# Pinning every engine's queue to the order in which a planner traces the kernel

## The chip, the cores and the metric

One core of a Trainium2 chip runs the whole program. Its engines are TensorE (PE, with its weight loads as PEld), VectorE (DVE), ScalarE (ACT), GpSimd (POOL) and SyncE (SP, which only issues DMAs here). Times are device microseconds (us) of one execution; lower is better.

## The reference

The input x has 32 rows (batch) of 128 tokens by 128 features, in float32. Two layers are added to it.

```python
x = x + L0_ffn(L0_cond(x, cond_512, ...), ...)
x = x + L1_ffn(L1_cond(x, ids, mask, cond_512, cond_64, fside, ...), ...)

# L0_cond: kx = modulated_linear(x); per token attention among 16 heads of 8
#          features, q = k = v = kx; then another modulated linear
# L0_ffn:  gates choose and weight experts out of 16 (at least the two best);
#          q, k, v = weighted sums over the chosen experts' projections;
#          attention over blocks of 256 tokens as reshaped; output projection
#          again by the same experts
# L1_cond: layer norms whose gain and shift are looked up by ids, three small
#          MLPs of the row's state, all joined in a last MLP and a layer norm
# L1_ffn:  top 2 of 8 experts, each silu(x W_gate) * (x W_up) through W_down
```

The kernel computes only the experts that are chosen. It counts whether more than two would be needed anywhere, and has a second version for that case, which does not run on these inputs.

## The kernel before, in words

The 32 rows are handled in 4 parts (p0 to p3) of 8 rows, and inside a part in groups of 4 rows (g0 to g7 over the whole batch). A part passes through these stages:

- *front0*, per group, on two lanes: the modulated linear and the per-token attention of layer 0's condition. Its large DVE operations are prod (scores) and prodv (weights times values), with a sum over prodv taken by PE transposes (pat).
- *gates0* and *route*: a chain of short DVE operations, with a matmul (prk) in it that ranks tokens. Its links after prk are blk, upto, first, row_at, pick, row_plf and at last place, the row of a sorted buffer to which every token goes. The same numbers, clamped, are back.
- *send*: 16 indirect DMAs from POOL that scatter the part's rows into rows_x in HBM, sorted by expert and padded to blocks of 128 rows, 28 blocks per part.
- *experts0*: SP loads the blocks (crx), PE transposes them (pcrx) and multiplies by the block's expert (qkv), ACT copies the result (yx), and SP writes it (outs_x).
- *attend0*, per row, on three lanes: POOL gathers both experts' results (gq), ACT and DVE weight and add them, PE does the attention (psc, ppT, pov), ACT copies (prT and others), and POOL scatters the result to rows_o.
- *output0*: blocks again, cro, yo, outs_o. Then *add_up*: POOL gathers (ygo), DVE adds to X.
- *front1*, per group, on two lanes, after all groups of front0: the condition of layer 1, from the transposes pyT to the logits pl.
- *gates1*, *route*, *send* to rows_c (crow is what is sent), *experts1* with loads crc, gate and up matmuls gu, their product hh, its transposes phT, the down matmuls yc and the writes outs_c, 22 blocks per part; and add_up again with ygc, after which SP writes the output.

Each stage is a Python generator. A planner, the class `Turns`, runs the one that by its own count can begin first, and the calls that the generator makes until its next `yield` are traced. Every call goes through a wrapper, which keeps that count (`account`, with a cost for each kind of instruction):

```python
def call(out, *args, **kw):
    turns.account(name, op, out, args, kw)
    return fn(out, *args, **kw)
```

All instructions are issued from the wrapper, so the profile gives nearly all of them the same line, L237; they are told apart by their tiles.

## Time and profile before

| | |
|---|---|
| median of 3 runs | 1030.94 us |
| lowest and highest | 1025.16 and 1032.98 us |
| the profiled execution: time | 1030.12 us |
| its span, from first to last instruction | 1028.2 us |
| granted TensorE clock, mean | 0.774 of full speed |
| PE, DVE, ACT, POOL busy | 618.9, 481.4, 392.0, 390.7 us |
| DMA | 118.24 MB, 115 GB/s over the span |

The busy time of an engine is the time in which at least one of its instructions ran. The slices in the page's second part each stand for a fortieth of the span, 25.7 us, and a digit gives the busy share in tenths. A wait line names the engine that waits and the tile that its next instruction writes, then what released it, the total, the number of times and the longest. A timeline line gives start and length in us, the engine, the operation, and in brackets the idle time ahead of it with its releaser. "Remote", and "another core or an unknown queue", mean that the profile shows no releaser.

### The profile page before, as it was taken

The numbers are of one execution on the slowest core, as the hardware profiler recorded it, in microseconds if no ns is written. First come the engines' busy times: TensorE is split into PE (matmuls) and PEld (weight loads), VectorE is DVE, ScalarE is ACT, GpSimd is POOL, SyncE is SP. The second block draws the span as 40 slices with busy tenths as digits, with TensorE's granted clock in tenths as the row PEclk, the third lists the DMA queues.
The fourth block names the chain that finished last, engine by engine and source line by source line (L and its number), as shares of the span: only waits on it lengthen the run. The fifth ranks groups of instructions, "written<-read, shape, count | busy, mean of one in ns | idle before, by whom it ended". The sixth has DMA issues, their size and how long they took to land.

```text
span 1028.2 us, 11024 instructions
## 1 busy us (share of the span) xinstructions
PE 618.9 (60%) x3050; PEld 435.7 (42%) x3050; DVE 481.4 (47%) x1625; ACT 392.0 (38%) x1016; POOL 390.7 (38%) x399
## 2 busy tenths in 40 slices
PE   5366536855962863555672583285959569469570
PEld 3245424543742642533451461173536346246340
DVE  6878772972893550022432454253646435032212
ACT  3232132714641452333662482162536225135240
POOL 0000061075027247365557457705321640741405
PEclk9976567965995886686886675678989789769885
DMA  8990014323324465554654342352121221232212
GB/s 231 322 266 1 0 31 143 134 81 108 133 103 128 123 202 170 145 172 138 208 174 133 105 139 62 117 158 73 65 74 49 60 78 54 79 102 59 66 51 61
DMA packets 144604, 118.24 MB, mean 115 GB/s; under 512 B 11416, under 2 KB 133720, under 8 KB 144536
## 3 DMA queue, kind: packets, MB, share of 16 engines
q1 hardware_dynamic: 130200, 83.88, 26.8%
q0 software_dynamic: 14336, 33.58, 11.2%
q8 instruction: 28, 0.46, 0.2%
q14 instruction: 40, 0.33, 0.1%
HBM read 57.38 MB, written 60.03 MB: 114 GB/s over the span
## 4 chain that ended last, share of the span: by engine, by line
PE 32%; issue 13%; DVE 13%; POOL 12%; another core or an unknown queue 10%; DMA 10%; ACT 5%; SPq 3%; POOLq 0%; ACTq 0%; DVEq 0%
POOL rows_x L237 6%; PE gu L237 5%; PE yc L237 4%; PE pat L237 3%; PE qkv L237 3%; DVE prodv L237 3%; SPq L237 3%; PE pre L237 2%; POOL gq L237 2%; PE phT L237 2%; DMA gq<-outs_x,back 2%; POOL rows_o L237 2%; PE yo L237 2%; POOL ygc L237 1%
## 5 line engine op out<-in xcount | busy, mean ns | idle before, releaser
L237 POOL DMA_INDIRECT rows_x<-h,place x64 | 70.1, 1095 | 202.9 <-DVE past L237 132.1
L237 POOL DMA_INDIRECT gq<-outs_x,back x64 | 68.6, 1072 | 146.5 <-PE pov L237 67.4
L237 POOL DMA_INDIRECT ygc<-outs_c,back x64 | 60.8, 949 | 127.9 <-DMA outs_c<-ycs 97.7
L237 PE MATMUL qkv<-w,crTx 128*128 x224 | 96.2, 545 | 14.6 <-issue 4.9
L237 PE MATMUL gu<-w1e,crTc 128*128 x176 | 100.0, 657 | 5.8 <-DVE hh L237 3.8
L237 POOL DMA_INDIRECT rows_c<-crow,place x64 | 62.1, 970 | 72.3 <-ACT hT L237 36.3
L237 PE MATMUL pat<-ident,prodv 128*128 128x128 f32 x512 | 70.5, 301 | 22.7 <-DVE prodv L237 17.6
L237 DVE TENSOR_TENSOR prodv<-S,kx 128x2048 f32<-128x2048 f32 x32 | 72.4, 2287 | 24.7 <-PE pat L237 24.6
L237 POOL DMA_INDIRECT ygo<-outs_o,back x64 | 61.2, 956 | 59.2 <-DVE hh L237 28.2
L237 PEld LDWEIGHTS pat<-ident,prodv 128*128 128x128 f32 x512 | 65.5, 157 | 29.6 <-issue 17.3
L237 DVE TENSOR_TENSOR hh<-hh,gu 128x256 f32<-128x256 f32 x88 | 36.6, 418 | 88.1 <-ACT hh L237 68.6
L237 POOL DMA_INDIRECT rows_o<-orow,place x64 | 65.5, 1024 | 19.5 <-issue 15.8
L237 PE MATMUL yc<-w1e,hT 128*128 x352 | 55.0, 299 | 24.1 <-ACT hT L237 19.9
L237 PEld LDWEIGHTS yc<-w1e,hT 128*128 128x128 f32 x352 | 49.9, 211 | 32.8 <-ACT hT L237 23.8
L237 ACT COPY yx<-qkv 128x384 f32<-128x384 f32 x112 | 50.4, 490 | 27.3 <-PE qkv L237 13.7
L237 PE MATMUL phT<-ident,hh 128*128 128x128 f32 x176 | 35.7, 292 | 38.3 <-DVE l1t L237 11.0
L237 DVE SCALAR_TENSOR_TENSOR gq<-gq,w 128x384 f32<-128x384 f32 x32 | 19.7, 616 | 81.7 <-DMA gq<-outs_x,back 36.2
L237 PEld LDWEIGHTS qkv<-w,crTx 128*128 128x128 f32 x224 | 41.9, 214 | 34.4 <-issue 13.4
L237 PEld LDWEIGHTS phT<-ident,hh 128*128 128x128 f32 x176 | 24.2, 151 | 69.8 <-issue 48.5
L237 ACT ACTIVATE hh<-gu 128x256 f32<-128x256 f32 x88 | 34.3, 390 | 47.0 <-PE phT L237 28.0
L237 PE MATMUL pcrx<-ident,crx 128*128 128x128 f32 x112 | 22.4, 329 | 46.2 <-DMA crx<-rows_x 44.9
L237 DVE TENSOR_REDUCE nm<-psc 128x1 f32<-128x128 f32 x32 | 9.2, 289 | 76.9 <-remote 24.1
(289 smaller groups left out, 1417.2 us busy)
## 6 DMA issues: line engine op xcount, KB each, us to landing
outs_x<-yx SPq DMA_DIRECT2D x56, 384.0 KB
crx<-rows_x SPq DMA_DIRECT2D x28, 256.0 KB
cro<-rows_o SPq DMA_DIRECT2D x28, 256.0 KB
outs_o<-yos SPq DMA_DIRECT2D x28, 256.0 KB
crc<-rows_c SPq DMA_DIRECT2D x20, 256.0 KB
outs_c<-ycs SPq DMA_DIRECT2D x20, 256.0 KB
rows_x<-zeros SPq DMA_DIRECT2D x6, 512.0 KB
rows_o<-zeros SPq DMA_DIRECT2D x6, 512.0 KB
```

What stands on the lines that cost most here:

```text
L237: return fn(out, *args, **kw)
```

## The change

At every call, before the new instruction is traced, a new method `pin` looks through what was traced since the last call. It gives each instruction on one of the five engines an edge to the instruction traced before it on the same engine. The edge is of order alone: no semaphore belongs to it. Within a group of scatters to the same buffer no edges are made; what follows the group has an edge to each of them. The wrapper calls `pin`, and `scatter` tells the planner its group. Nothing else changes: not the calls, their sizes, the buffers or the planner's costs.

```diff
+    ENGINES = {
+        getattr(mybir.EngineType, n) for n in ("PE", "Activation", "DVE", "Pool", "SP")
+    }
...
-    def __init__(self, nc):
+    def __init__(self, tc):
+        nc = self.nc = tc.nc
+        self.tc, self.seen, self.last, self.groups = tc, 0, {}, {}
...
                 def call(out, *args, **kw):
+                    turns.pin()
                     turns.account(name, op, out, args, kw)
                     return fn(out, *args, **kw)
...
+    def pin(self):
+        traced = self.nc.cur_bb.bb.instructions
+        for i in traced[self.seen:]:
+            if i.engine not in self.ENGINES:
+                continue
+            group = self.groups.get(i.name)
+            before, run, of = self.last.get(i.engine, ([], [], None))
+            if group is None or group != of:
+                before, run = run, []
+            for name in before:
+                self.tc.add_manual_dep(
+                    i, name,
+                    mybir.DependencyInfo(mybir.DependencyClass.NoSync, mybir.DependencyReason.DATA),
+                    reason="in the order of tracing",
+                )
+            self.last[i.engine] = before, run + [i.name], group
+        self.seen = len(traced)
...
-    tn = Turns(nc)
+    tn = Turns(tc)
...
         tc.add_to_no_dep_group(group, ins.ins)
+        tn.groups[ins.ins.name] = group
```

The instructions are the same 10690 before and after; they stand in another order on all five engines.

## The prediction

> **What bounds the kernel now.** I read the page's busy line first, then the waits, then the chain of work that ended last, then engine timelines where a wait was long.

> ```profile
> PE 618.9 (60%) x3050; PEld 435.7 (42%) x3050; DVE 481.4 (47%) x1625; ACT 392.0 (38%) x1016; POOL 390.7 (38%) x399
> DVE  6878772972893550022432454253646435032212
> ...
> PE 32%; issue 13%; DVE 13%; POOL 12%; another core or an unknown queue 10%; DMA 10%; ACT 5%; SPq 3%; POOLq 0%; ACTq 0%; DVEq 0%
> ```

> No engine is full: the busiest, PE, works 60% of the span. DVE's slices of 25.7 us say that for the first 12, to about 300 us, it is 7 to 9 tenths busy, and later 2 to 6. The chain passes through every engine. So the time is set by when one stage hands over to the next, which is what an order decides. The waits name the hand-overs (us in total, times, longest):

> ```profile
> POOL rows_x L237 <- DVE past L237: 132.1, 1, 132.1
> POOL ygc L237 <- DMA outs_c<-ycs: 97.7, 3, 37.5
> ...
> POOL gq L237 <- issue: 63.7, 49, 49.0
> ...
> PE pcrx L237 <- DMA crx<-rows_x: 44.9, 4, 21.2
> ```

> POOL can't scatter part 0's rows until DVE has routed them at 134 us, and the expert matmuls can't start until the rows have come back. The end of part 0's routing, in DVE's timeline (start, length):

> ```profile
> 123.97 0.17 DVE L237 CAST blk<-blk_i 128x16 f32<-128x16 int32 x1
> 124.45 2.29 DVE L237 TENSOR_TENSOR prodv<-S,kx 128x2048 f32<-128x2048 f32 x1 [0.31 <-PE pat L237]
> 126.66 0.18 DVE L237 TENSOR_TENSOR_SCAN upto<-blk 128x16 f32<-128x16 f32 x1
> 126.76 1.33 DVE L237 TENSOR_TENSOR prod<-kx 128x1152 f32<-128x1152 f32 x1
> 128.01 0.17 DVE L237 TENSOR_TENSOR first<-upto,blk 128x16 f32<-128x16 f32 x1
> ...
> 134.08 0.17 DVE L237 CAST place<-row_plf 128x16 uint32<-128x16 f32 x1
> ```

> Each short link of the route waits behind a 1.3 to 2.3 us operation of the next group's attention, which nobody needs yet: 10.1 us from blk to place. Part 3's route, with less beside it, takes 381.80 to 384.17, or 2.4 us, for the same links. The timelines of PE, DVE and ACT after 400 us show the other kind of loss:

> ```profile
> 416.70 0.79 PE L237 MATMUL pov<-gq,prT 128*128 128x128 f32 x2 [10.70 <-ACT prT L237]
> ...
> 417.18 0.62 DVE L237 SCALAR_TENSOR_TENSOR gq<-gq,w 128x384 f32<-128x384 f32 x1 [13.47 <-ACT prT L237]
> ...
> 415.88 0.62 ACT L237 ACTIVATE gq<-gq,w 128x384 f32<-128x384 f32 x1 [11.70 <-DMA gq<-outs_x,back]
> ```

> Here ACT's queue holds the scaling of a gather (gq) ahead of prT, a copy whose input was there at 404. The gather sits on POOL behind part 3's scatter. PE, DVE and ACT all stand for 10.7 to 13.5 us.

> [...] one copy with its input ready waited 11.7 us behind its predecessor. So an order fixed badly costs as much as one fixed well saves. [...] part 0's last scatter record starts at 157.35 and lasts 0.96, and the chain carries another 2.24 us of DMA up to 160.9. [...] rows_x scatters have a mean of 1095 ns, those of part 0 reaching 2.02 us beside DVE's attention, while ygc gathers have 949 ns.

> **The change part by part.** [...] The added edges are of order alone on one engine, so they put no new wait into the program; their cost is only what stands behind whom. I sum against the profiled execution, 1030.12 us (span 1028.2); the median of the three runs, 1030.94, is 0.8 above it and I ignore that.

> *Routing of the first layer.* I listed what stood ahead of each part's place on DVE and no longer does, with durations from the trace: 19.0 us for part 0 (four prodv of 2.3, prod and S of 1.3 each, a softmax of 3.0), 13.8 for part 1, 13.7 for part 2, 5.0 for part 3; nothing is newly ahead. Of part 0's 19.0 I count 17: about 2 us of DVE's idle time comes to light as the links hop to PE and back (the chain shows 0.99 us of "issue" at 114.3 for one such hop). Part 0's place falls from 134.1 to about 117. The work moved behind it fits beside the scatter and the load, 31 us (135.1 to 166.0) paced by POOL and the DMA queues. Expert matmuls start at about 149 instead of 166.

> *PE and SP there.* The next group's pk and pkx (138 to 143 before) now stand behind the first experts' transposes. They wait for rows that land at about 146, so they lose some 5 us, inside the 24 us that part 1 gains. SP now issues the second layer's weight loads (5.8 MB) and the zero fills of rows_c between the first loads of experts; at the 231 to 322 GB/s of the first slices 5.8 MB are 18 to 25 us of DMA, spread over a stretch at 69 GB/s. I take 3 us; the bounds are 0 and 20.

> *POOL, parts 0 to 2.* Before, part 1's scatters (221.6) stood behind six gathers that waited 49 us for outs_x. Now twelve of the sixteen stand ahead. With place at about 190, twelve at 1.27 us (0.96 and a gap of 0.30) end at 206, so gq of row 0 comes at 207: no gain against 208.6. The other four end at about 215 instead of 244.6. Part 2's sixteen still stand before gq of row 4, but come about 38 us earlier, so part 0's attention, which ended at 387, does too, and its output experts start near 360 instead of 398.6.

> *The second layer's start.* It gets back only part of this. The gathers for the residual (ygo of rows 1 to 3 of part 0, run at 449 to 462) now stand behind gathers of part 2, row 3's behind one run at 503.4 to 505.7. If those come 38 us early, ygo of row 3 ends near 470 and front1's first group starts some 14 us earlier than 486. With the later groups, for which POOL is less in the way, I carry 24 us into the second layer.

> *Second layer.* front1's eight groups run on two lanes from 486 to 867, a group taking 52 to 92 us from its first transpose to its logits, and the last route (872.1) follows them. On PE the instructions traced ahead of part 2's and part 3's place are 33.0 and 29.4 us (summed durations, which overlap) less than what had run by then. The page's busy time is about 0.6 of such sums, so 18 us less stands ahead of the last route: 18 us. The stall at 404 goes, since the prT concerned is traced ahead of that gather: 13 us, of which nothing is sure to remain if the gather itself is late next.

> *Tail.* What no longer stands ahead must run after: 18 us of PE work, in a tail where PE was busy 75.7 of 128 us after 900; I let 10 of it show. The last scatter on POOL (14 of part 3's 16) moves behind part 1's sixteen ygc gathers, from 875.6 to after about 920 less the shift. Its rows were needed at 941.7 when gu of part 3 began, and 14 times 1.27 plus 3 to land is 21: in balance with PE, which was at part 2 until 938. I take 0, bounds 0 and 20.

> Sum: -24 - 18 - 13 + 10 = -45; 1030 - 45 = 985 us.

> **The rivals.** *Slower: the front of the second layer dams up the experts on PE.* gu 15 of part 0 ran at 761.9, while the logits of front1's group 5 (pl), now traced ahead of it, ran at 792.8. PE will have to wait for them. Nothing is lost if that group comes 31 us earlier; if it gains only the first route's 17, all expert work behind is 14 us late, and the displaced PE work adds to the tail: 1030 + 14 + 4 = 1048 us; with no gain 1065. For it: 31 us of ready matmuls filled PE's gaps before. Against it: front1's own instructions lose the same work ahead of them.

> *Nothing measurable.* The gain goes into the waits at ygo and at ygc (97.7 us), which end with transfers: 1030. For it: gq of row 0 gains nothing by the sum above. Against it: every route is freed, not one.

> *More.* 10% of the chain has no visible releaser; from 556.15 DVE stands 15.26 us for the largest of these pieces, and the reduction that ends it, at 571.43, had its input at 567.1. If such stalls come from the mixture of POOL's bursts with waiting queues, and the order dissolves half of these 103 us as well, the time is 985 - 50 = 935 us. Nothing shown ties them to the order.

> That the edges do nothing is no case: the queues differ in hundreds of places.

> **How the numbers follow.** Forecast 985 with its own range 955 to 1015: 0.50. More gain: 0.12. Nothing: 0.11. Slower: 0.27. Within 1% is about what a measurement of this kernel can tell from no change, 1021 to 1041. The range 930 to 1055 takes in both rivals' centres and leaves out some 0.07 below and 0.11 above. Faster 0.62, same 0.11, slower 0.27.

> **What would show it.** Right: place of part 0 near 117 with its links 0.2 to 0.5 us apart; first qkv near 149; part 1's scatter ending near 215; no common gap of PE, DVE and ACT of over 10 us near part 3's scatter; the last route near 820. Wrong: front1's first group no earlier than 486, gu of part 0 waiting on pl for over 15 us, or PE idle before part 3's first gu for its rows.

## The result, and the profile after

The changed kernel takes 1020.12 us (median of 20 runs, 1014.31 to 1029.15) against 1029.38 us for the kernel before beside it (20 runs, 1022.02 to 1035.77). The ratio is 0.9915, with a 95% interval of 0.9889 to 0.994: a gain of 0.85%, real but a fifth of the 45 us that were forecast. The profiled execution has a span of 1012.8 us, 15.4 less than before.

The page of the kernel after, in the order in which before was read: busy time, DVE's slices, the shares of the chain that ended last.

```profile
PE 637.9 (63%) x3050; PEld 447.2 (44%) x3050; DVE 526.7 (52%) x1625; ACT 394.9 (39%) x1016; POOL 398.9 (39%) x399
DVE  6797986979976500121454463566666534221312
...
DVE 27%; PE 26%; another core or an unknown queue 15%; issue 13%; ACT 8%; SPq 4%; DMA 4%; POOL 3%; ACTq 0%; DVEq 0%; POOLq 0%
```

POOL and DMA, 12% and 10% of the chain before, are down to 3% and 4%. What has grown is time with no visible releaser: 153 us of the chain against 106 before. The 47 us more are as much as the forecast gain. In a second pair of traces of the two kernels (further down) it grows from 89 to 116 us: the direction is the same, the size is not. The waits that the lists put down to "remote" agree: they add up to 172.6 us before and 213.1 after, in the second pair to 155.1 and 193.6. Some lines of the list after (us in total, times, longest):

```profile
POOL rows_x L243 <- DVE past L243: 118.9, 1, 118.9
DVE hh L243 <- ACT hh L243: 91.1, 50, 13.9
POOL ygc L243 <- DMA outs_c<-ycs: 69.5, 3, 29.3
...
POOL rows_c L243 <- ACT ycs L243: 51.9, 1, 51.9
...
DVE l0st L243 <- remote: 33.0, 2, 23.7
```

The start-up wait is 13.2 us shorter, as forecast in kind. The largest "remote" wait stands where a DVE chain of front1 (l0st) begins.

In the first layer the order did what was expected of it. The end of part 0's route in DVE's timeline:

```profile
116.25 1.22 DVE L243 TENSOR_REDUCE hm<-S 128x64 f32<-128x1024 f32 x1
117.50 1.22 DVE L243 TENSOR_TENSOR S<-S,hm 128x1024 f32<-128x1024 f32 x1
118.64 0.17 DVE L243 TENSOR_SCALAR blk_i<-prk 128x16 int32<-128x16 f32 x1
...
119.05 0.17 DVE L243 CAST blk<-blk_i 128x16 f32<-128x16 int32 x1
119.26 0.19 DVE L243 TENSOR_TENSOR_SCAN upto<-blk 128x16 f32<-128x16 f32 x1
119.49 0.17 DVE L243 TENSOR_TENSOR first<-upto,blk 128x16 f32<-128x16 f32 x1
...
120.93 0.17 DVE L243 CAST place<-row_plf 128x16 uint32<-128x16 f32 x1
```

From blk to place it is now 1.9 us instead of 10.1, with the same links next to each other. Start times from the timelines of the two kernels, by stage:

| | before | after | difference |
|---|---|---|---|
| place of part 0 | 134.1 | 120.9 | -13.2 |
| place of part 1 | 214.0 | 195.5 | -18.5 |
| place of part 2 | 301.3 | 269.1 | -32.2 |
| place of part 3 | 384.2 | 343.8 | -40.4 |
| first cro of part 0 | 398.6 | 355.4 | -43.2 |
| pyT of the first front1 group | 486.4 | 490.4 | +4.0 |
| second layer's place, part 0 | 629.9 | 602.0 | -27.9 |
| part 2 | 811.9 | 763.1 | -48.8 |
| part 3 | 872.1 | 841.1 | -31.0 |
| last ygc gather | 1018.7 | 1005.2 | -13.5 |

The lead grows to 43 us, is lost before front1 starts, comes back, and falls to 13.5 us in the last two stretches. The largest wait without a releaser stands in the middle of part 3's output and front1. ACT's timeline there:

```profile
616.85 1.14 ACT L243 ACTIVATE act<-pre,b1T 128x128 f32<-128x128 f32 x4 [4.67 <-PE pre L243]
617.86 1.65 ACT L243 ACTIVATE xk<-X,l1nb,l1y 128x128 f32<-128x128 f32 x4
621.12 0.59 ACT L243 COPY q<-pyT 128x512 f32<-128x512 f32 x1 [1.62 <-remote]
630.98 0.59 ACT L243 COPY crTo<-pcro 128x512 f32<-128x512 f32 x1 [9.27 <-remote]
640.22 0.59 ACT L243 COPY q<-pxh 128x512 f32<-128x512 f32 x1 [8.66 <-remote]
```

and in DVE's at the same time:

```profile
640.16 0.30 DVE L243 BATCH_NORM_STATS2 l0st<-py 128x6 f32<-128x128 f32 x1 [23.67 <-remote]
```

PE's timeline has what they wait for:

```profile
617.53 0.66 PE L243 MATMUL pcro<-ident,cro 128*128 128x128 f32 x4 [0.29 <-DMA cro<-rows_o]
...
619.37 0.22 PE L243 MATMUL py<-b2row,ones_b 96*128 96x128 bf16 x1
```

PE's last matmul into py ends at 619.59. DVE, with nothing else to do since 616.49, starts to read py at 640.16: 20.6 us after its input was complete by the record. ACT reads pcro 12.8 us after its matmuls ended at 618.19, though it was free from 621.71. SyncE, whose next cro load waits until PE has read cro for that same pcro, goes on at 630.97 too. So it is the signal of PE that comes late, not one engine that sleeps.

The trace shows this directly, since it also keeps the time of each semaphore update: each wait of ACT and DVE above that is put down to "remote" ends 0.02 us after an update of PE's, so that update is the signal here. Taken in the order of PE's queue, the update for pcro, due at 618.19, is recorded at 630.96, and the one for py, due at 619.59, at 640.14. The next four, due between 622.88 and 634.54, follow within 0.27 us.

Some updates are missing from this trace: 613 of PE's 718 are on record, and all engines and DMAs together have 7594, where a trace of the same kernel without late signals (below) has 13634. The first of PE's to go missing, 3 of 18, are due between 100 and 150 us, and POOL's first sixteen indirect DMAs run there, from 122.0 to 148.0.

To count the late starts, I call a start late if the instruction begins over 1 us after both the end of the last instruction whose signal it waits for and the end of the instruction before it on its engine. The sums add up over engines and need not lie on the critical chain, and they depend on how the source of a signal is found: if it is taken to be the last PE instruction on the same tile, the 250.3 us of the changed kernel's first trace in the table below become 191.4 and its third trace stays at 0.

### The profile page after: what moved, and what is told of

Its sections match the earlier page's. It is cut to its first block, busy times and chain, and to the rows that moved or that the text cites. A ratio compares the mean times of both kernels' runs of the same rounds, so it can differ in the third digit from the quotient of the medians.

```text
span 1012.8 us, 11074 instructions
## 1 busy us (share of the span) xinstructions
PE 637.9 (63%) x3050; PEld 447.2 (44%) x3050; DVE 526.7 (52%) x1625; ACT 394.9 (39%) x1016; POOL 398.9 (39%) x399
## 4 chain that ended last, share of the span: by engine, by line
DVE 27%; PE 26%; another core or an unknown queue 15%; issue 13%; ACT 8%; SPq 4%; DMA 4%; POOL 3%; ACTq 0%; DVEq 0%; POOLq 0%
PE gu L243 5%; SPq L243 4%; PE pat L243 3%; PE qkv L243 3%; PE yc L243 3%; DVE S L243 3%; DVE prodv L243 2%; POOL rows_x L243 2%; DVE prod L243 2%; PE phT L243 1%; DVE X L243 1%; PE pre L243 1%; DVE l1t L243 1%; DVE l0t L243 1%
## 5 line engine op out<-in xcount | busy, mean ns | idle before, releaser
L243 POOL DMA_INDIRECT rows_x<-h,place x64 | 80.3, 1255 | 219.1 <-DVE past L243 118.9
L243 POOL DMA_INDIRECT ygc<-outs_c,back x64 | 60.8, 950 | 123.7 <-DMA outs_c<-ycs 69.5
L243 POOL DMA_INDIRECT gq<-outs_x,back x64 | 66.1, 1032 | 59.6 <-PE pov L243 40.1
L243 PE MATMUL yo<-w,crTo 128*128 x224 | 38.2, 331 | 43.3 <-ACT crTo L243 27.9
L243 ACT COPY yx<-qkv 128x384 f32<-128x384 f32 x112 | 49.8, 487 | 20.8 <-PE qkv L243 11.0
L243 PE MATMUL phT<-ident,hh 128*128 128x128 f32 x176 | 35.9, 293 | 33.8 <-ACT hT L243 17.6
L243 PEld LDWEIGHTS yo<-w,crTo 128*128 128x128 f32 x224 | 34.7, 238 | 47.3 <-ACT crTo L243 29.9
L243 PEld LDWEIGHTS phT<-ident,hh 128*128 128x128 f32 x176 | 23.4, 149 | 69.5 <-issue 31.5
```

## The experiments

The chips that the runs fell on are of two kinds, and the numbers can't be read without this: on some the kernel before takes about 1022 to 1029 us, on others about 947. Every trace from the former has late signals, none from the latter has, so I call them chips with and without late signals. No chip on record came back at another time, so it is not shown whether the kind belongs to the chip or to the occasion. Every ratio is to the kernel before on the same chip at the same time.

| kernel | chips with late signals | chips without |
|---|---|---|
| before | 1029.4; 1022.8; 1028.2 us | 947.7; 948.2; 947.5 us |
| changed | 0.9915 [0.9889, 0.994]; 0.9901 [0.9869, 0.9932] | 0.9415 [0.9388, 0.9443] |
| first layer's edges only | not run | 0.9768 [0.9733, 0.9803]; 0.9784 [0.9746, 0.9822] |
| second layer's edges only | not run | 0.9868 [0.9823, 0.9913]; 0.9855 [0.9822, 0.9887] |
| rows_c scatters at once | 1.0017 [0.9986, 1.0048] | 0.9344 [0.9306, 0.9381] |
| no edges on POOL | 1.0047 [1.0014, 1.008]; 1.0026 [1.0001, 1.0051] | not run |
| plain DMAs in place of half the indirect ones | 0.861 (one execution) | 0.9038 [0.9002, 0.9074]; 0.9044 [0.9016, 0.9071]; 0.906 [0.8983, 0.9138]; 0.902 (one execution) |

Late starts whose last signal is PE's and whose waiter is another engine, from the trace of each run:

| kernel | chip | late starts | sum, us | after 600 us |
|---|---|---|---|---|
| before, first trace | with | 57 | 246.7 | 154.9 |
| before, again | with | 48 | 240.7 | 167.9 |
| changed, first trace | with | 50 | 250.3 | 148.8 |
| changed, again | with | 49 | 234.9 | 135.7 |
| rows_c at once | with | 60 | 248.5 | 136.7 |
| no edges on POOL, second | with | 67 | 240.6 | 112.3 |
| plain DMAs | with, same as the line above | 11 | 48.6 | 0.0 |
| before, third | without | 1 | 1.3 | 0.0 |
| changed, third | without | 0 | 0.0 | 0.0 |

The semaphore updates say the same without any matching of instructions. In the eleven traces from chips without late signals, every update of PE on record comes within 35 ns of the end of an instruction that signals. In the eight from the other chips, 19 to 78 come over 1 us after the last such end (56 of 613 in the changed kernel's first trace). In these eight DVE has 3 to 20 of them as well, up to 3.9 us late, and ACT none.

**Which half of the order.** The edges are made only while front1 has not begun, or only from then on. Theory A was that the second layer's order gives back what the first gained; theory B that late signals take it whichever order stands.

```diff
+        self.layer = 0
...
-            if i.engine not in self.ENGINES:
+            if i.engine not in self.ENGINES or self.layer != 0:     # or != 1
                 continue
...
         yield ("S",)
+        tn.layer = 1
         ids = f1.tile([P, 3, GT], I32, tag="S", name=f"ids{g}")
```

> Edges of order only for what is traced before the first group of front1; all later instructions are left to the scheduler as in the kernel before. Theory A (the order of the second layer gives back what the first layer gained: front1 dams the experts on PE, the scatters of rows_c stand behind ygc): the first layer's gain of 40 us at part 3's place stays, and the time is 990 to 1005 us. Theory B (the gain is lost to something that neither order avoids, the late starts while POOL issues its indirect DMAs): no better than the changed kernel, 1015 to 1030 us.

> The reverse: the first layer is left to the scheduler, edges only from the first group of front1 on. Theory A: slower than the kernel before, 1040 to 1055 us. Theory B: the second order is as good as the scheduler's, so about as before, 1022 to 1035 us. If the gain that is left comes from the second layer: 1015 to 1020 us.

924.61 us against 947.73 (0.9768), and 934.08 (0.9868). The absolute numbers of the expectation are for the other kind of chip and can't be compared; the ratios can. The second layer's order alone gains 1.3%, so theory A falls on these chips. It falls in another way too: with the second layer left to the scheduler, the lead of 34 us at part 3's place (347.3 against 381.2 in the kernel before on such a chip) is down to 24 us at the last route (777.7 against 801.7). Both were repeated on another chip of that kind.

> Edges for the first layer alone, again. On the chip with late signals: theory A (the second layer's order gives back the gain) 0.965 to 0.98 of before; theory B (late signals take it, whichever order) 0.985 to 1.0. On the other chip 0.977 again.

> Edges for the second layer alone, again. On the chip with late signals: theory A 1.01 or more of before; theory B 0.99 to 1.005. On the other chip 0.987 again.

0.9784 and 0.9855. The two halves gain 2.2 and 1.4%, 3.6% together, while the whole, beside the repeats on the same chip, gains 5.9%: the halves help each other. A likely reason, not tested, is that the second layer starts from what the first delivers. Neither half was run on a chip with late signals.

**The changed kernel itself, on both kinds of chip.**

> The changed kernel, unaltered, beside the kernel before on the same chip. The kernel before took 1029 us where the change was first measured and 948 us where the last four runs were made, and in those four no signal of PE was late. If the late signals took the gain: where they are absent, the changed kernel is faster by what its two halves gave alone there (2.3% and 1.3%), 3 to 5% in all, 900 to 920 us against 948. If the order itself gives the gain back: within 1.5% of the kernel before there too.

> The kernel before, unaltered, for its trace on this chip. Where it takes about 948 us: the late starts behind PE's signals, 200 us of waits in the first trace, are gone, below 30 us. Where it takes about 1029: they are there again.

1011.09 us against 1022.75 (0.9901) on a chip with late signals; the unaltered kernel before stands at 1.000 there, and its late starts are there again: of the 32 that were over 4 us late in its first trace, 27 came at the same instructions. This is no noise, but something the program meets at the same places.

> The changed kernel once more. On the chip where the kernel before takes about 1023 to 1029 us: 0.985 to 0.995 of it, as twice before. On the chip where it takes 948 us and no signal of PE is late: 0.95 to 0.97 of it (900 to 920 us) if the late signals took the gain, 0.985 or more if the order itself gives it back.

892.28 us against 948.16 (0.9415), 55.9 us less, which is more than the 0.95 to 0.97 that were expected. In this trace no start behind PE's signal is late. ACT's timeline for the same instructions as at 616.85 above:

```profile
559.75 1.14 ACT L243 ACTIVATE act<-pre,b1T 128x128 f32<-128x128 f32 x4 [4.17 <-PE pre L243]
560.77 1.65 ACT L243 ACTIVATE xk<-X,l1nb,l1y 128x128 f32<-128x128 f32 x4
562.30 0.58 ACT L243 COPY q<-pyT 128x512 f32<-128x512 f32 x1
563.44 0.59 ACT L243 COPY crTo<-pcro 128x512 f32<-128x512 f32 x1 [0.55 <-PE pcro L243]
566.10 0.59 ACT L243 COPY q<-pxh 128x512 f32<-128x512 f32 x1 [2.07 <-PE pxh L243]
```

From act to the second q it is 6.4 us here and 23.4 us there, with the same queue.

> The kernel before, unaltered, for its trace. On the chip where it takes 948 us: late starts behind PE's signals below 30 us in all, the queues the same, and the 75 us against the other chip are found in those waits. On the chip with late signals: as before, 1023 us.

947.75 us; one late start behind PE, of 1.3 us. The spans are 1028.2 and 945.2 us for the kernel before (83.0 less without late signals), 1012.8 and 890.6 for the changed one (122.2 less). So a chip with late signals costs the changed kernel 39 us more than the kernel before. Up to part 3's place the two kinds of chip agree within 3 us for either kernel (384.2 and 381.2 before, 343.8 and 340.9 after), and no start before 330 us is late in the changed kernel's first trace; that the chips differ in nothing else is not shown.

**Does POOL's work make the signals late?** In the changed kernel's first trace 245.6 of the 250.3 us lie inside runs of indirect DMAs on POOL (gaps below 0.6 us, and 3 us after the end), which cover 60% of the span. But none is before 330 us, though three runs of 16 to 26 lie there. These runs cover so much that this alone proves little. To test it, half of the indirect DMAs were taken off POOL:

```diff
     def gather(dst, src, place, k, t):
+        if src.shape[1] == P:                # ygo and ygc
+            at = bass.IndirectOffsetOnAxis(ap=place[:, k, t:t + 1], axis=0)
+            tn.pin()
+            tn.account("POOL", "indirect_dma_start", dst, (None, src, at), {})
+            b = 2 * t + k
+            nc.sync.dma_start(dst, src[b * P:(b + 1) * P, :])
+            return
...
     def scatter(dst, place, k, t, src, group):
+        if group[0] == "c":                  # rows_c, likewise
...
```

One more small DMA of place on SyncE, ahead of each part's sixteen, keeps them waiting for the route.

> The changed kernel with the rows_c scatters and the ygo and ygc gathers (192 of 384 indirect DMAs) replaced by plain DMAs of the same bytes, issued by SynC at the same place of the trace; rows go to and come from fixed places, so the routing of these rows is left out. Theory B (signals of PE and DVE arrive late while POOL issues indirect DMAs): late starts after 600 us, over 1 us after the last signal was due, vanish and the time falls to 940 to 985 us. Theory A, or late starts with another cause: they stay, and the time is within 15 us of the changed kernel.

> rows_c, ygo and ygc as plain DMAs from SyncE to and from fixed places, their routing left out. On the chip with late signals: if POOL's indirect DMAs make them late, late starts after 600 us shrink from some 100 us to below 20 and the time is near 925 us or less; if not, above 970 us. On the others 855 us again.

The first four runs of it fell on chips without late signals: 854.39, 856.39, 856.01 and 853.52 us, 0.902 to 0.906 of before, with no late starts behind PE to take away. Neither of the first expectations fits this, since both were made for the other kind of chip. On the chip where both were run it is 856.39 against 892.28 us, so 4% on top of the changed kernel is what the plain DMAs save by themselves; where they save it is not shown.

The fifth fell on a chip with late signals, beside the kernel without edges on POOL: 885.5 us against 1028.15 for the kernel before. The late starts after 600 us are 112.3 us in the kernel beside it and 0.0 here; the 48.6 that remain lie before 600, where POOL still has its other half. The time expected was 925 or less if POOL's DMAs cause them, above 970 if not. The missing updates agree: none of PE's, ACT's or DVE's is missing after 600 us, while 69 of PE's are before. So where the indirect DMAs are gone the late signals are gone: shown for these 192 DMAs, by one execution. What makes PE's signals wait on these chips is not shown, nor why no start before 330 us is late, although in the changed kernel's first trace 16 of PE's 81 updates due between 200 and 300 us are already missing, where POOL's runs lie at 196.4 to 236.4 and 269.6 to 303.8. One rival is untested: every execution on record has a span and a clock from the profiler, and the late signals and the missing records come together, so the recording itself may have a part in the delay.

**POOL's order in the second layer.** Part 2's place was ready at 763.1, 48.8 us early, but its scatter ended at 824.5, 12.3 early, since twelve of its scatters stand behind part 0's ygc gathers. POOL's timeline shows the start of the scatter:

```profile
764.04 0.96 POOL L243 DMA_INDIRECT rows_c<-crow,place  x1 [51.90 <-ACT ycs L243]
```

Two runs tried to take that back. One traces all 16 scatters of a part in one go:

```diff
-            yield
+            if kind != "c":
+                yield
+        yield
```

> The changed kernel, but all 16 scatters of a part's rows_c are traced in one go, so they stand ahead of the ygc gathers on POOL. If POOL's order set the tail (part 2's scatter ended at 824 us though its place was ready at 763; part 3's at 911 with place at 841): crc of parts 2 and 3 come 25 to 40 us earlier and the time falls to 1000 to 1010 us. If PE, busy with part 1 until 863 and part 2 until 923, sets the tail: no change, 1015 to 1023 us.

> All 16 scatters of rows_c in one go, again, now beside the changed kernel itself. If POOL's order was what the second layer lost: 15 to 30 us less than the changed kernel in this call. If the 885 us of before belong to the chip: the same as the changed kernel, within 8 us.

885.19 us against 947.73 (0.9344) without late signals, 1024.81 against 1022.75 (1.0017) with them, where the changed kernel on the same chip has 0.9901. So the version that is fastest on one kind of chip, some 0.7% ahead of the changed kernel (on different chips), loses all the gain on the other. Neither expectation of the second run came true: it is 13.7 us slower than the changed kernel beside it. The late starts sum to 248.5 us against 234.9 there. Part 2's scatter does end earlier (796.7 against 823.3), but part 3's place comes later (872.4 against 840.0; 770.1 against 744.8 on the chips without late signals). Why the time is longer on one kind of chip alone is left open.

The other leaves POOL's queue to the scheduler:

```diff
-        getattr(mybir.EngineType, n) for n in ("PE", "Activation", "DVE", "Pool", "SP")
+        getattr(mybir.EngineType, n) for n in ("PE", "Activation", "DVE", "SP")
```

> Edges on all engines but POOL, whose queue is left to the scheduler. If the traced order of POOL is the harmful part (rows_c behind ygc, gathers for the residual late): 10 to 25 us faster than the changed kernel in this call. If POOL's order carries the first layer's gain (part 1's scatter ahead of gq): 5 to 20 us slower.

> Edges on all engines but POOL. On a chip without late signals the changed kernel takes 0.9415 of before and loses at rows_c behind ygc (part 2: place at 682 us, its scatter ended at 738; part 3: 745 and 811). If POOL's order is a net loss: 0.925 to 0.937. If POOL's order carries the first layer's gain: 0.945 to 0.965. On the chip with late signals: 1.005 again.

1026.85 us (1.0047), and 1032.22 us against 1028.15 (1.0026) on another chip of that kind: in the first case 16 us slower than the changed kernel on the same chip. With late signals POOL's traced order is a gain on the whole, in spite of the tail; without it the rest of the order is worth nothing there. It was not run on a chip without late signals.

## Why the prediction was wrong

The forecast was 985 us, 0.956 of its base; the measured ratio is 0.9915. The measured time lies inside the wide range but outside the 955 to 1015 of the likeliest case, and the rival "nothing measurable", at 0.11, came closest, though not for its reason: the wait at ygc did not take up the gain, it fell from 97.7 to 69.5 us.

*The step that failed: the time without a releaser was taken as fixed.* The prediction had these 106 us in its view, but its sum has no term for them; they appear only in the case "more", as something that the order might dissolve. They grew instead, to 153 us in the chain (89 to 116 in the second pair). The sum has two checkpoints that show the effect: the last route was to come 55 us earlier (24, 18 and 13), and the tail was to give back 10.

| | forecast | with late signals (first traces) | without (third traces) |
|---|---|---|---|
| place of part 3, first layer | not given | -40.4 | -40.3 |
| last route | -55 | -31.0 | -56.9 |
| tail, from there to the last ygc gather | +10 | +17.6 | +4.5 |

Both checkpoints are about met where signals come in time, and both are missed where they don't. The late starts are no more in sum than before (246.7 and 250.3 us). That more of them lie on the path, since engines that used to wait for routes and gathers now wait for PE, is argued from the sums and not tested by itself.

That the total fits where signals come in time, 55.9 us against 45, is in part luck, as the parts show:

- *Routing of the first layer: right in kind, mis-sized at the start.* Place of part 0 came at 120.9, not 117, and the first qkv at 155.6, not 149. From raw, a copy of ACT ahead of the gates, to place it is 13.4 us instead of 34.2, so more than the 17 us were won there. But raw of part 0 ended at 107.5 instead of 99.9: nothing new stood ahead of place on DVE, but small operations that prepare weights (the splits of gain, b and bias) stood ahead of the first groups' prod, which ran until 37.4 instead of 31.6. I had listed what stands ahead and not in which order it stands.
- *Parts 1 to 3: near.* Place of part 1 came at 195.5 (190 was forecast), that of part 2 came 32.2 us earlier (38); part 1's scatter ended at 225 instead of 215. Part 0's output experts started at 355.4; 360 was forecast.
- *The stall at 404: wrong.* It did not go, it moved. DVE's timeline has it beside part 3's scatter, first on a chip with late signals, then on one without:

```profile
399.82 0.62 DVE L243 SCALAR_TENSOR_TENSOR gq<-gq,w 128x384 f32<-128x384 f32 x1 [44.93 <-ACT gq L243]
...
381.18 0.62 DVE L243 SCALAR_TENSOR_TENSOR gq<-gq,w 128x384 f32<-128x384 f32 x1 [26.93 <-DMA gq<-outs_x,back]
```

  In the first trace the gather that it needs ran at 377.5, behind all of part 3's scatter; ACT's scaling stood behind copies of output0, one of which was 16.9 us late behind PE's signal. The 13 us of the sum were there on neither kind of chip.
- *front1's start: wrong in sign for the first group.* It came at 490.4 against a forecast of 472, though the second and third groups came 20.8 and 23.3 us earlier, near the 24 that were carried. Late signals are not the main cause: pyT to its reader was 4.2 us late there, and without late signals the first group came only 4.2 us earlier (461.8 instead of 466.0). The gathers of ygo did stand behind part 2's gathers as stated. With the first layer's edges alone, also without late signals, the first group starts at 409.5: it is the order of what is traced from front1 on that holds it back.
- *Second layer's rate: more than was counted.* From the first pyT to the last route it is 35 us less with late signals (350.7 instead of 385.7) and 52.7 less without; 18, and 13 for the stall, were counted.
- *Tail: the sign was right, the size too small with late signals.* From the last route to the last ygc gather it took 146.5 us before and 164.1 after. Part 3's rows_c cost little: its scatter ended 18 us later than before (911.0 against 893.0), as stated, and the gap between part 2's last gu and part 3's first grew from 3.4 to 6.2 us.
- *The slower rival.* The trace corrects its place: pl of group 5 stands behind gu 15 and ahead of gu 16. They ran at 753, 754 and 755, so the two chains meet on PE as the rival had it, but group 5 came 38.4 us earlier than before, past the 31 from which it costs nothing.
- *Scatters beside DVE's attention: named, but not in the sum.* Scatters to rows_x that overlap a prod, a prodv or an S<-S,hm on DVE take 1.50 us on average before and 1.48 after; the others take 0.97 and 0.98. Before, 15 of the 64 overlap one, after, 35, and POOL's time for all of them rises from 70.1 to 80.3 us. So the price of the new order on POOL was larger than the nothing that was counted.
- *Readings that were off, without weight in the sum.* The last scatter of part 0 starts at 158.61; 157.35 is the one before it. Its transfer ends at 160.85, 1.28 us after its record ends at 159.57. The longest scatter of part 0 took 2.19 us, not 2.02. And the edges did not leave the waits quite as they were: the page counts 11074 instructions after and 11024 before, and the 50 more are separate waits on semaphores. What they cost is not shown.

## What to carry to other kernels

List the time that the profile gives to no releaser and find which signals are behind it before you price a reordering: here such time grew when the schedule got tighter, and on the chips that have it most of the gain was missing. The planner's order was worth 6% where signals came in time, more than its two halves together. Measure such a change on more than one chip, because 0.94 and 0.99 were both true.

## What the runs showed of the hardware

- On some chips signals of PE came late. In the changed kernel's first trace, between 618 and 641 us, SyncE went on 12.8 us, ACT 12.8 and 17.3 us, and DVE 20.6 us after the matmuls that they waited for had ended by the record. The late starts behind PE sum to 250.3 us in this trace and to 234.9 in a second one of the same kernel. In the kernel before, 27 of the 32 late starts over 4 us came at the same instructions in a second trace. DVE's own updates were up to 3.9 us late in the eight traces from such chips, ACT's never over 1 us. In the eleven traces from other chips no update of PE came over 35 ns after its instruction. The kernel before took 1022.8 to 1029.4 us on the former and 947.5 to 948.2 on the latter.
- In the changed kernel's first trace six signals of PE, taken in the order of its queue and due between 618.19 and 634.54, were recorded at 630.96 and, five of them, from 640.14 to 640.41.
- In the same trace, from a chip with late signals, 7594 updates are on record; in the same kernel's trace without late signals 13634 are.
- With the indirect DMAs of the second layer issued as plain ones, late starts after 600 us were 0.0 us in one execution on a chip with late signals, against 112.3 us in the kernel beside it, and no update of PE, ACT or DVE was missing there.
- Replacing 192 indirect DMAs by plain ones, the routing left out, took 4% off the changed kernel even where no signal was late (856.39 against 892.28 us).
- A scatter to rows_x on GpSimd that overlapped a prod, a prodv or an S<-S,hm on VectorE took 1.48 to 1.50 us on average, up to 2.95, in the first two traces; the others took 0.97 to 0.98, none over 1.23.
